# Where the Mamba scan's operands come from: DMA spreads delta over the states, three PSUM tiles for the inputs, and GpSimd weights the inputs of 4 of 16 pairs

## The chip, the cores and the metric

The kernel runs on one core of a Trainium2 chip. The metric is the device time of one execution in microseconds (us); lower is better. A core has five engines that run their own instruction streams in order and wait for each other through semaphores: TensorE (PE, matrix multiply; PEld in the profile is its weight load), VectorE (DVE), ScalarE (ACT), GpSimd (POOL) and SyncE (SP, which here only issues DMAs). SBUF is the working memory of 128 partitions; PSUM is where PE writes, and in this kernel POOL works on SBUF only.

## The reference, cut to what matters

Four layers work on four images of 56 x 56 pixels with 128 channels: windowed attention, a Mamba block (the change is here), additive attention with a mixture of experts, and softmax attention with a second mixture. All is fp32. The Mamba layer takes each image row as a sequence of 56 steps:

```
u = silu(conv(h @ in_w)) ; dt, Bm, Cm = split(u @ xw)
delta = softplus(dt @ dtw + dtb)        # one number per step and channel, 256 channels
A = -exp(A_log)                         # 256 channels x 16 states
h_t = exp(delta_t * A) * h_(t-1) + delta_t * u_t * B_t       # 256 x 16 states
y_t = sum over states of h_t * C_t
out = (y + u * D) * silu(res) @ out_w   # and twice: NL = 2 such layers
```

## The kernel before, in words

**Tiling of the Mamba stage (function layer1).** A chunk is 448 steps: 8 image rows of one image (CH = 448, 7 chunks an image). One *block* is one chunk in one of the two Mamba layers, so there are 4 x 7 x 2 = 56 blocks. A block has 256 channels x 16 states = 4096 recurrences, which are 32 tiles of 128 partitions (8 channels x 16 states) by 448 steps. They are worked two at a time: a *pair* is 128 x 896, and a block has PAIRS = 16 pairs, the stage 896.

**One pair before.** The order is written by hand, in a loop over p (lines 864 to 875), and each engine takes its instructions in that order:

- `select` (L739): PE makes `a` = delta times rate, spread over states (`decays`, L723, against the table `A_pick`), and `u` = delta*u spread over states (`spread_inputs`, L732, against the 0/1 table `pick`). `a` is one PSUM tile of two banks, `u` two such tiles. `decays` is for pair p+1 where `spread_inputs` is for pair p; the two use different groups of 32 rows of PE.
- ACT makes E = exp(a) from PSUM to SBUF (L748).
- `inputs` (L753): DVE multiplies u by B in place, in PSUM.
- `scan` (L760): DVE runs the recurrence over E (SBUF) and u (PSUM) into `hs` (SBUF, 7 buffers); then POOL multiplies hs by C in place (L765).
- `sums` (L771): PE adds up the states of two pairs into `y`, issued at every odd p for the pairs p-5 and p-4.

**Around a block.** `mamba_pre` (L877) prepares the next block at fixed pair numbers of the running one: conv (L889), silu (L901), the projection (L907), delta, B and C (L918 to L932), du = delta*u on POOL (L936, after pair 8), and two POOL memsets that put 1e30 at the first step of each row, so that exp gives 0 and the recurrence restarts (L939). `gate` (L787, POOL), `project` (L796, L804) and `pass_on` finish the previous block. m and y in PSUM have one bank each; with a (2 banks) and u (4) all eight banks are in use.

**Queues.** All DMAs are issued by SP, in an order that a scheduler sets; the other engines' order is as written. In the Mamba stage SP has nothing to do. Ahead of it, in layer 0, SP loads everything: the tables, the weights (`layer1_weights`, L605 to 639), and then images 1 to 3 (`load_image`, L127). Image 1 is normalised early in layer 0 (L184).

## Time and profile before

| what | value |
| --- | --- |
| three timed runs | 7893.22, 7884.90, 7877.51 us; median 7884.9 |
| span of the profiled execution | 7883.1 us, 1.8 us under that median |
| busy over the span: PE, DVE, ACT, POOL | 6718.3, 6070.7, 4990.0, 2552.6 us |
| first and last scan start (L760) | 650.8 and 3529.3 us |
| one pair in between | (3529.3 - 650.8) / 895 = 3.216 us |
| one block of 16 pairs | 51.46 us |
| DMA traffic | 102.35 MB, mean 13 GB/s |

The page gives busy time by engine, then 40 slices of the span with busy shares in tenths, the chain of work that ended last, and groups of instructions with their count, busy time, the mean duration of one in ns, and the idle time of the engine just before them with what released it. The view by windows gives each engine's busy time in a stretch, the granted PE clock, the DMA engines' mean busy share and their GB/s. The timeline gives start, duration, engine, line, operation and operands; x4 means four merged instructions, and brackets show idle time ahead and who ended it.

### The profile page before, as it was taken

The page shows a single profiled execution, that of the slowest core. Times are in us where ns is not written, and L with a number is a line of the kernel's source. Part 1 is how long each engine was busy: PE and PEld are TensorE (multiplying, and loading weights), DVE is VectorE, ACT ScalarE, POOL GpSimd, SP SyncE. Part 2 cuts the span into 40 slices and gives each one's busy share as a digit, 9 for nine tenths or more (in the row PEclk, how much of TensorE's full clock was granted, in tenths as well). Part 3 has the DMA queues.
Part 4 walks back from the last instruction along what each step waited for, and adds up shares of the span by engine and source line. Part 5 has one row for each costly group of instructions (what it writes and reads, how often), then busy time and mean ns, then how long its engine had stood idle before and what let it go on. Part 6 is the DMA issues. An engine that isn't in the chain of part 4 may idle for free.

```text
span 7883.1 us, 105890 instructions
## 1 busy us (share of the span) xinstructions
PE 6718.3 (85%) x41081; PEld 2672.6 (34%) x41081; DVE 6070.7 (77%) x10241; ACT 4990.0 (63%) x4903; POOL 2552.6 (32%) x1911
## 2 busy tenths in 40 slices
PE   7888989998999899987777777777777889999999
PEld 3452333333333333322222222222222344444544
DVE  5787999999999999997877887877787755344434
ACT  4455555555555655548998899899889953333332
POOL 4455777777777777760000000000001000000000
PEclk8998999999999999999999999899999989999999
DMA  3000000000000000000000000000003101210000
GB/s 63 6 2 1 1 1 1 1 1 1 1 1 1 1 1 1 1 3 2 1 1 1 5 1 1 1 5 1 1 32 114 47 6 47 91 57 5 5 5 6
DMA packets 86479, 102.35 MB, mean 13 GB/s; under 512 B 21368, under 2 KB 51414, under 8 KB 85463
## 3 DMA queue, kind: packets, MB, share of 16 engines
q1 hardware_dynamic: 85975, 95.58, 4.2%
q8 instruction: 322, 5.28, 0.3%
q14 instruction: 182, 1.49, 0.1%
HBM read 85.28 MB, written 10.29 MB: 12 GB/s over the span
## 4 chain that ended last, share of the span: by engine, by line
PE 35%; DVE 33%; ACT 20%; issue 7%; POOL 1%; DVEq 0%; DMA 0%; ACTq 0%; SPq 0%; POOLq 0%
DVE hs L760 17%; ACT th L1149 13%; PE q L1707 7%; PE o L1718 7%; DVE u L753 6%; PE s L1160 6%; DVE th L1140 4%; PE o L1187 2%; PE pe L1872 2%; ACT E L748 2%; PE a L723 2%; PE m L889 2%; DVE e L488 1%; ACT L748 1%; PE y L771 1%
## 5 line engine op out<-in xcount | busy, mean ns | idle before, releaser
L1149 ACT ACTIVATE th<-th 128x3136 f32<-128x3136 f32 (+12 forms) x1120 | 2293.6, 2093 | 194.6 <-DVE th L1140 138.4
L1140 DVE TENSOR_SCALAR th<-fT,g 128x784 f32<-128x784 f32 (+6 forms) x3920 | 1918.4, 556 | 482.2 <-PE s L1160 449.9
L765 POOL TENSOR_TENSOR hs<-hs,bc 128x896 f32<-128x896 f32 x896 | 1867.3, 2084 | 793.5 <-DVE hs L760 761.3
L1160 PE MATMUL s<-th,place 128*32 128x392 f32 (+7 forms) x14336 | 1489.2, 492 | 667.8 <-ACT th L1149 664.8
L760 DVE TENSOR_TENSOR_SCAN hs<-E,u 128x896 f32<-128x896 f32 x896 | 1810.1, 2020 | 117.9 <-ACT E L748 1.9
L748 ACT ACTIVATE E<-a 128x896 f32<-128x896 f32 x896 | 821.5, 917 | 806.3 <-PE u L732 333.7
L723 PE MATMUL a<-delta,A_pick 32*128 32x448 f32 x3584 | 983.2, 601 | 148.0 <-ACT E L748 140.4
L753 DVE TENSOR_TENSOR u<-u,bc 128x896 f32<-128x896 f32 x896 | 964.2, 1076 | 63.9 <-PE u L732 63.5
L732 PE MATMUL u<-du,pick 32*128 32x448 f32 x3584 | 975.2, 601 | 35.8 <-DVE hs L760 35.7
L1160 PEld LDWEIGHTS s<-th,place 128*32 128x32 f32 (+1 forms) x14336 | 425.7, 111 | 1612.1 <-ACT th L1149 1082.4
L1712 ACT ACTIVATE e<-q,shift 128x448 f32<-128x448 f32 (+1 forms) x700 | 441.4, 633 | 748.6 <-PE q L1707 748.2
L1178 POOL TENSOR_TENSOR e<-e,later 112x112 f32<-112x112 f32 x112 | 80.2, 716 | 2311.9 <-ACT e L1171 1670.1
L1718 PE MATMUL o<-e,xk 128*128 128x448 f32 (+1 forms) x1400 | 653.1, 548 | 25.7 <-ACT oT L1693 25.7
L1877 DVE SCALAR_TENSOR_TENSOR X<-pe,r_gate,X 112x128 f32<-112x128 f32 x896 | 314.0, 351 | 455.3 <-PE pe L1872 419.7
L1707 PE MATMUL q<-xT 128*128 128x448 f32 (+1 forms) x1400 | 654.7, 550 | 2.3 <-ACT e L1712 2.2
L723 PEld LDWEIGHTS a<-delta,A_pick 32*128 32x128 f32 x3584 | 295.7, 188 | 697.4 <-ACT E L748 466.5
L771 PE MATMUL y<-hs,sum 128*32 128x448 f32 x3584 | 443.9, 566 | 4.4 <-POOL hs L765 4.4
L1187 PE MATMUL o<-e,xa 112*128 112x392 f32 (+5 forms) x1024 | 424.3, 537 | 1.1 <-POOL e L1178 1.1
L1718 PEld LDWEIGHTS o<-e,xk 128*128 128x128 f32 (+1 forms) x1400 | 262.2, 191 | 310.5 <-issue 275.5
L732 PEld LDWEIGHTS u<-du,pick 32*128 32x128 f32 x3584 | 295.5, 188 | 200.0 <-DVE hs L760 183.9
L1707 PEld LDWEIGHTS q<-xT 128*128 128x128 f32 (+1 forms) x1400 | 249.0, 189 | 238.1 <-issue 213.0
L1806 POOL MEMSET lc_xa<- 112x4 f32 x28 | 3.1, 110 | 889.5 <-DVE lc_xa L1800 519.5
(254 smaller groups left out, 7186.2 us busy)
## 6 DMA issues: line engine op xcount, KB each, us to landing
wide<-in_L_ffn_weight SPq DMA_DIRECT2D x64, 1024.0 KB
X<-in_x SPq DMA_DIRECT2D x8, 784.0 KB
out<-X SPq DMA_DIRECT2D x28, 224.0 KB
M<-wide SPq DMA_DIRECT2D x4, 784.0 KB
wide<-M SPq DMA_DIRECT2D x4, 784.0 KB
e_edge<-dtab SPq DMA_DIRECT2D x42, 49.0 KB
cw<-in_L_conv_conv_w SPq DMA_DIRECT2D x4, 256.0 KB
c_h<-in_L_ffn_weight SPq DMA_DIRECT2D x16, 64.0 KB
```

The source lines that it names most:

```text
L723: nc.tensor.matmul(halves(to)[:, k], w["A"][own, order[j][2], f, q, :], pre[j]["delta"][own, f], start=True, stop=True,)
L732: nc.tensor.matmul(halves(to)[:, k], w["pick"][own, q, :], pre[j]["du"][own, f], start=True, stop=True,)
L748: nc.scalar.activation(E[p + 1], t, AF.Exp)
L753: nc.vector.tensor_mul(v, v, pre[p // PAIRS]["bc"][:, 0:1].to_broadcast([P, 2, CH]))
L760: nc.vector.tensor_tensor_scan(flat, E.pop(p), V.pop(p), 0.0, op0=ALU.mult, op1=ALU.add)
L765: nc.gpsimd.tensor_mul(HS[p], HS[p], bc[:, 1:2].to_broadcast([P, 2, CH]))
L1140: nc.vector.tensor_scalar(th[i][:, blk, lo:hi], fT[j][:, lo:hi], im[order[j][0]]["g"][:, at : at + 1], None, op0=ALU.add,)
L1149: nc.scalar.activation(own, own, AF.Tanh)
L1160: nc.tensor.matmul(ps[j, J][QW * blk : QW * blk + rows, h, lo:hi], place[:, off : off + rows], z[:, blk, h * HALF + lo : h * HALF + hi], s ...
L1187: nc.tensor.matmul(po[j][:, h, lo:hi], im[b]["xa"][:, J, :], e[:, h * HALF + lo : h * HALF + hi], start=(J == 0), stop=(J == t + ((h + 1) ...
L1707: nc.tensor.matmul(ps[:n, :CH], xT[b][:, k : k + n], xT[b][:, c * CH : (c + 1) * CH], start=True, stop=True,)
L1718: nc.tensor.matmul(po[b, c], xk[b][:n, t, :], es.pop((b, c, t))[:n], start=(t == 0), stop=(t == N - 1))
```

## The change

It does four things. The state index becomes the outer part of the partition number (`% DG`, `// DG` instead of `// DS`, `% DS` in the tables), so that the 8 channels of a tile are 8 rows, repeated 16 times. `mamba_pre` writes delta and du of each block to DRAM (8 DMAs), and `fetch` reads for each pair 8 rows x 3584 bytes into 128 partitions (one DMA of 448 KB, each row read 16 times): delta for 12 pairs, du for 4. For the 12 pairs ACT applies the rate as a per-partition scale, exp(rate * delta), in two halves in place in SBUF, and PE makes only u. For the pairs 0, 3, 7 and 12 of a block PE makes only a, ACT exponentiates it in place in PSUM, and POOL multiplies the fetched du by B in SBUF; the scan then reads E from PSUM and the input from SBUF. PSUM's six banks are three tiles of one kind. `rate` is a new table, loaded in layer 0 by 32 DMAs of 8 x 32 single numbers, ahead of images 1 to 3.

```diff
+POOL_PAIRS = (0, 3, 7, 12)
+DG = P // DS
+ROW_END = 8
...
-        pick[:, q, :] = (p % HD // 8 == q)[:, None] & (p[None, :] // DS == p[:, None] % 8)
-        back[p, q, 8 * q + p // DS] = 1.0
+        pick[:, q, :] = (p % HD // DG == q)[:, None] & (p[None, :] % DG == p[:, None] % DG)
+        back[p, q, DG * q + p % DG] = 1.0
...
+        w["rate"] = self.t(wp, [P, NL, DI // DG], "rate")
+        by_state = a["L1_conv_A_log"].rearrange("l (g d) n -> n l d g", d=DG)
+            for n in range(DS):
+                own = slice(n * DG, (n + 1) * DG)
+                for l in range(NL):
+                    nc.sync.dma_start(out=w["rate"][own, l], in_=by_state[n, l])
...
+        def rate():
+            nc.scalar.activation(w["rate"], w["rate"], AF.Exp)
+            nc.vector.tensor_scalar(w["rate"], w["rate"], -1.0, None, op0=ALU.mult)
...
-            ps_a = ctx.enter_context(tc.tile_pool(name="l1_a", bufs=1, space=PSUM))
-            ps_u = ctx.enter_context(tc.tile_pool(name="l1_u", bufs=2, space=PSUM))
+            dr = ctx.enter_context(tc.tile_pool(name="l1_dram", bufs=2, space=DRAM))
+            ps_u = ctx.enter_context(tc.tile_pool(name="l1_u", bufs=3, space=PSUM))
...
+            on_pool = lambda p: p % PAIRS in POOL_PAIRS
+            inside = lambda p: 0 <= p < n_pairs
+            def fetch(p):
+                j, f, q, r0 = place(p)
+                if on_pool(p):
+                    to, of = V, pre[j]["du_dram"]
+                    to[p] = self.t(sm, [P, 2 * CH + ROW_END], "V")[:, : 2 * CH]
+                else:
+                    to, of = D, pre[j]["delta_dram"]
+                    to[p] = self.t(sm, [P, 2 * CH + ROW_END], "E", bufs=5)[:, : 2 * CH]
+                rows = of[f, r0 // 2, q * DG : (q + 1) * DG].rearrange("d k t -> d (k t)")
+                nc.sync.dma_start(
+                    out=to[p],
+                    in_=rows.unsqueeze(0).to_broadcast([DS, DG, 2 * CH]),
+                )
             def select(p):
-                if 0 <= p + 1 < n_pairs:
-                    t = two_banks(ps_a, "a")
-                    decays(p + 1, t)
-                if 0 <= p < n_pairs:
-                    V[p] = two_banks(ps_u, "u")
-                    spread_inputs(p, V[p])
-                if 0 <= p + 1 < n_pairs:
-                    E[p + 1] = self.t(sm, [P, 2 * CH], "E", bufs=3)
-                    nc.scalar.activation(E[p + 1], t, AF.Exp)
-            def inputs(p):
-                if 0 <= p < n_pairs:
+                j, f, q, r0 = place(p)
+                u = two_banks(ps_u, "u")
+                if on_pool(p):
+                    decays(p, u)
+                    nc.scalar.activation(u, u, AF.Exp)
+                    E[p] = u
+                    return
+                spread_inputs(p, u)
+                V[p] = u
+                E[p] = D.pop(p)
+                for k in range(2):
+                    e = halves(E[p])[:, k]
+                    g = (f * QG + r0 + k) * QG + q
+                    rate = w["rate"][:, order[j][2], g : g + 1]
+                    nc.scalar.activation(e, e, AF.Exp, scale=rate)
+            def inputs(p, eng):
+                if on_pool(p) == (eng is nc.gpsimd):
                     v = halves(V[p])
-                    nc.vector.tensor_mul(
+                    eng.tensor_mul(
                         v, v, pre[p // PAIRS]["bc"][:, 0:1].to_broadcast([P, 2, CH])
                     )
...
-                if p >= -2:
-                    select(p + 1)
-                if 0 <= p < n_pairs:
+                if inside(p + 4):
+                    fetch(p + 4)
+                if inside(p + 2):
+                    select(p + 2)
+                    inputs(p + 2, nc.gpsimd)
+                if inside(p + 1):
+                    inputs(p + 1, nc.vector)
+                if inside(p):
                     scan(p)
...
-                inputs(p + 1)
...
+            for of in ("delta", "du"):
+                to = r[of + "_dram"] = dr.tile([NHALF, 2, HD, 2, CH], F32, tag=of, name=of + "_dram")
+                for i in range(4):
+                    nc.sync.dma_start(
+                        out=to[:, i // 2, :, i % 2].rearrange("f c t -> c f t"),
+                        in_=r[of][i * HD : (i + 1) * HD],
+                    )
```

More of the change, by code (lines that the diff above doesn't have):

```diff
@@ L95, in host_constants @@
         "k_out": back_out,
-        "k_state": (p[None, :] % DS == np.arange(DS)[:, None]).astype(np.float32),
+        "k_state": (p[None, :] // DG == np.arange(DS)[:, None]).astype(np.float32),
         "k_pick": pick.reshape(P, QG * P),
@@ L624, in layer1_weights @@
         )
+        w["rate"] = self.t(wp, [P, NL, DI // DG], "rate")
+        by_state = a["L1_conv_A_log"].rearrange("l (g d) n -> n l d g", d=DG)
+        with nc.allow_non_contiguous_dma(reason="a small table, by state and channel"):
+            for n in range(DS):
+                own = slice(n * DG, (n + 1) * DG)
+                for l in range(NL):
+                    nc.sync.dma_start(out=w["rate"][own, l], in_=by_state[n, l])
         xw = self.load(
@@ L649, in rates @@
             nc.vector.scalar_tensor_tensor(
-                w["A"][:, l, f, q, :].rearrange("p (j n) -> p j n", n=DS),
-                w["pick"][:, q, :].rearrange("p (j n) -> p j n", n=DS), -1.0,
-                A[:, l, f, :].unsqueeze(1).to_broadcast([P, P // DS, DS]),
+                w["A"][:, l, f, q, :].rearrange("p (n j) -> p n j", n=DS),
+                w["pick"][:, q, :].rearrange("p (n j) -> p n j", n=DS), -1.0,
+                A[:, l, f, :].unsqueeze(2).to_broadcast([P, DS, DG]),
                 op0=ALU.mult, op1=ALU.mult,
@@ L664, in layer1_weights @@
         bind = lambda f, *args: lambda: f(*args)
-        steps = [lambda: nc.scalar.activation(A, A, AF.Exp)]
+        def rate():
+            nc.scalar.activation(w["rate"], w["rate"], AF.Exp)
+            nc.vector.tensor_scalar(w["rate"], w["rate"], -1.0, None, op0=ALU.mult)
+        steps = [lambda: nc.scalar.activation(A, A, AF.Exp), rate]
         steps += [
@@ L703, in layer1 @@
             h = {}
-            pre, yg, E, V, HS, py = {}, {}, {}, {}, {}, {}
+            pre, yg, E, D, V, HS, py = {}, {}, {}, {}, {}, {}, {}
             def hand_over(b, g):
@@ L848, in layer1 @@
                 add(last, at + 12, skip, j, 1)
-                head, tail = self.mamba_pre(pre, j, block, h, w, sm, m)
+                head, tail = self.mamba_pre(pre, j, block, h, w, sm, m, dr)
                 for steps, to in ((head, first), (tail, last)):
@@ L874, in layer1, with mamba_pre @@
                     step()
-                inputs(p + 1)
-    def mamba_pre(self, pre, j, block, h, w, sm, m):
+    def mamba_pre(self, pre, j, block, h, w, sm, m, dr):
         nc = self.nc
```

## The prediction

> **What bounds the kernel now.** I read the page first (busy shares, slices), then the windows of the Mamba stage, then its groups of instructions and its timeline.

> ```profile
> DVE  5787999999999999997877887877787755344434
> ```
> ```profile
> 1500.00:2000.00 500.00, 455.77 (x2324) 157.98 (x2316) 476.53 (x333) 277.69 (x341) 363.86 (x211) 0.96 0.00 1
> 2000.00:2500.00 500.00, 463.84 (x2344) 162.84 (x2344) 477.27 (x321) 286.02 (x347) 370.06 (x211) 0.96 0.00 1
> ```
> Columns of the windows: length, then busy us of PE, PEld, DVE, ACT, POOL, granted PE clock, DMA share, GB/s. DVE is busy 95% through the stage; POOL is idle a quarter of it, ACT 43%, the DMA engines all of it. PE shows 92%, but see below: much of that is order, not need.

> ```profile
> 2002.92 1.07 DVE L753 TENSOR_TENSOR u<-u,bc 128x896 f32<-128x896 f32 x1
> 2004.13 2.02 DVE L760 TENSOR_TENSOR_SCAN hs<-E,u 128x896 f32<-128x896 f32 x1
> 2006.07 1.07 DVE L753 TENSOR_TENSOR u<-u,bc 128x896 f32<-128x896 f32 x1
> ```
> Read start to start. The multiply holds DVE for 1.21 us (the scan waits for its result); the scan for 1.94, because the next multiply, which doesn't need it, starts 0.09 before its end. So a pair costs 3.15, a block 16 x 3.145 = 50.3, plus 0.95 of other DVE work (the remaining groups of 1000 to 3300 us: 42.6 us over 44.7 blocks) = 51.3. Measured: 51.46. DVE alone sets the stage's 56 x 51.46 = 2882 us.

> **The change, part by part, for one block.**

> *DVE.* Four multiplies leave. The other twelve now stand before the scan of the pair ahead, which doesn't need them; by the 0.09 overlap above they hold DVE 1.07 - 0.09 = 0.98, not 1.21. Sum: 16 x 1.94 + 12 x 0.98 + 0.95 = 43.8. If the 0.23 of wait stays, 46.5. I take 43.8: the scan-to-multiply step shows independent neighbours.

> *POOL.*
> ```profile
> 2006.29 2.08 POOL L765 TENSOR_TENSOR hs<-hs,bc 128x896 f32<-128x896 f32 x1 [1.05 <-DVE hs L760]
> 2008.33 1.13 POOL L787 TENSOR_TENSOR yg<-yg,sres 128x448 f32<-128x448 f32 x1
> 2009.44 2.08 POOL L765 TENSOR_TENSOR hs<-hs,bc 128x896 f32<-128x896 f32 x1
> ```
> The bracket on the first line is the slack: over 1 us in most pairs. Back to back, hs costs 2.04, yg 1.11, du with its memsets 2.24 (2024.04 to 2026.28). Now: 16 x 2.04 + 2 x 1.11 + 2.24 + 0.06 = 37.2. Added: 4 x 2.04 = 8.2 for the same shape. Sum 45.4: **POOL is the new longest engine**, 1.6 above DVE. The multiplies are worth 4 x 0.98 = 3.9 on DVE and cost 8.2 on POOL; they pay because POOL had 14 us idle.
> [...]

> *PE.* A pair's u alone takes 0.95 (four instructions at 2032.62, the next work at 2033.57); a and u together took 0.96 where they ran on different rows at once (2025.04 to 2026.00). So dropping one of the two saves PE little. Floor: 16 x 0.95 + 8 x 0.89 (sums) + 6.8 (conv) + 1.8 (xw) + 3.8 (dbl) + 1.9 (res) + 1.9 (D) + 3.4 (projection) = 42.0. `select(p+2)` waits for the third PSUM tile, released by scan p-1; DVE wants u after scan p. Laying the PE work out by pair number, PE is late for pair 4 by about 1.0 (convs at pairs 0 and 1 fill it, and pair 3 has no multiply to cover) and within 0.4 at pairs 2, 8, 9 and 13.

> *ACT.* 12 x (2 x 0.63 - 0.92) = +4.1 (0.63 is the row of a half with a per-partition operand, L897), on 29.4: 33.5 of 46. It works two pairs ahead, so the table loads stay covered, tightly at pair 9 after softplus.

> *DMA and SP.* Per block 16 fetches of 459 KB and 0.92 MB written: 8.3 MB in 46 us = 180 GB/s. Rows, none of this very kind:
> ```profile
> 228.00:229.00 1.00, 1.00 (x14) 0.59 (x12) 0.64 (x1) 0.78 (x2) 0.61 (x1) 1.00 0.55 139
> 229.00:230.00 1.00, 1.00 (x18) 0.40 (x18) 1.00 (x2) 0.80 (x1) 1.00 (x1) 1.00 0.45 123
> ```
> This is one load of 256 KB that reads one 2 KB row into all 128 partitions (`cw`, issued at 227.25): 1.0 us of all engines together, 262 GB/s while they run, all landed 2.75 us after issue. The 512-byte rows of the images reach 217 to 225. So the engines have room (share about 0.69 at 262). SP issues 24 DMAs x 0.35 = 8.4 of 46. The fetches are issued several pairs ahead (five E buffers), so their landing (2.75, plus 0.8 for the larger size = 3.5) is hidden, except at the block's start: du on POOL (after pair 8), 8 writes (2.8), landing 1.9 (the last `dtab` store at 25.02, the load that waits for it at 26.88), fetch 3.5, one fetch queued ahead 1.8: 10.0. POOL meanwhile has hs 9 to 13, one input multiply and yg: 13.5. Cover 3.5; if it is lost, each us over it stalls POOL once per block, 56 us in all.

> *Sum of the stage.* POOL 45.4 and DVE 43.8 with PE's 1.0 on it = 44.8 are nearly level and coupled: an input multiply stands in POOL's queue two pairs before its scan, so POOL can lag by only two to three pairs. I add 1.3 to the longer for that and for the waits, a choice of mine (today DVE loses 0.2 of 51.3 with POOL slack; two nearly level engines must lose more, and PE's lateness alone is 1.0): **46.7**. Saved 56 x (51.46 - 46.7) = 267. Bounds: 45.4 (339 saved) and 49.5 (110 saved, rival 1).

> *Layer 0.*
> ```profile
> 65.65 0.98 PE L184 MATMUL m<-ident,X 112*128 112x112 f32 x4 [13.89 <-DMA X<-in_x]
> ```
> Every engine already stands for 14 us because image 1 comes late. The 32 `rate` loads are ahead of it in SP's queue; the small loads after it (L977, L978) follow each other in 0.46: +15, with DMA work of 8192 four-byte packets beside it. Bounds: 32 x 0.31 = 10, and by the page's mean packet (4.2% of 16 x 7883 us over 85975 packets = 62 ns) 32 us on 16 engines, 63 if only half take part. I take 16, unhidden. The pipeline's first fill has cover: du ends at 626.8, the first scan is at 650.8, and writes, fetch and multiply need 12.

> *Total.* 7883.1 - 267 + 16 = 7632 of span; with the 1.8 us around it **7634**.

> **Rivals.**

> 1. *PE or ACT, or the chain at the block's start, takes the place of DVE* (a smaller gain). For: PE's floor of 42.0 has waits on ACT in it, ACT runs 5 us in one go around its table loads, cover at the start is 3.5. With 48 to 49.5 a block: 110 to 194 saved, 16 to 20 lost: 7705 to 7800. Against: three PSUM tiles, two pairs of lead.

> 2. *The fetches don't come fast enough* (slower). Place: the 16 DMA engines; a block is 128 packets of 3584 bytes for each and 32 half as long, 144 in all. It costs nothing until 144 packets take longer than 46.7 (324 ns each) and makes the kernel slower from 51.2 (355 ns, 161 GB/s). At 380 ns a block is 54.7: +181 + 16 = 8080. For: no row has 8 rows read 16 times each from freshly written DRAM, for 2.6 ms on end. Against: `cw` read one row 128 times at 125 ns for 2 KB (1.0 x 16 / 128), 219 ns for 3584 bytes by proportion; even the 512-byte rows reach 217 GB/s.
> [...]

> 3. *DVE and POOL hold each other up.*
> ```profile
> L225 DVE TENSOR_TENSOR gn_q<-gn_q,gn_ve 128x1 f32<-128x1 f32 x3 | 5.9, 1955 | 0.1
> ...
> L753 DVE TENSOR_TENSOR u<-u,bc 128x896 f32<-128x896 f32 x714 | 768.4, 1076 | 15.7 <-PE u L732 15.4
> ```
> A one-element multiply of two SBUF operands took 1.96 us beside a busy POOL, 0.16 in layer 0 with POOL idle. If the four scans with their input in SBUF were held like that, 4 x 2 = 8 a block: 54.7, 8080 again. Against: they still have one operand in PSUM, as L753 has, and that is not held. The few such small operations cost at most 20 us in all.

> **How the numbers follow.** Forecast 68%: 7560 to 7700, likeliest 7634. Rival 1 17%: 7705 to 7800. Rival 2 8%, rival 3 4%: near 8080. Left 3%: below 7560, or no change. The range 7560 to 7800 leaves out rivals 2 and 3 and that rest. Faster by over 0.2% (16 us, about what a measurement can tell from no change) 86%, within 2%, slower 12%.

> **What would show it.** Right: POOL busy about 97% in the stage, DVE about 93%, DVE's waits before scans ended by POOL's V at pairs 0, 3, 7 and 12; scans still 2.02 and POOL's multiplies still 2.08; DMA share 0.5 to 0.7 at 180 GB/s; the idle time before L184 near 30. Wrong: DVE's idle time ended by a DMA (rival 2) or by u of PE or E of ACT (rival 1), scans longer than 2.02 (rival 3), POOL's idle time before its input multiply ended by a DMA (the block's start).

## The result and the profile after

The changed kernel is **slower**: 7961.18 us median of 4 runs (7955.61 to 7963.58) against 7889.06 (7877.51 to 7897.53) of the kernel before; ratio 1.0092, 95% interval 1.0077 to 1.0106. The profiled execution has a span of 7960.8 us, 77.7 more than before. First and last scan stand at 659.7 and 3601.4: the Mamba stage took 2941.7 us, 63.2 more, and a block (2941.7 / 895 x 16) 52.6 us instead of 51.46. Another 8.9 us are lost ahead of the first scan, 5.6 behind the last.

Of the page after, the busy tenths of PE and DVE and the granted PE clock in 40 slices (the Mamba stage is slices 4 to 18):

```profile
PE   6888888888888888887777777777777889999999
...
DVE  5886888888888887887877887887787755444434
...
PEclk8997888788878887878999999999999989999999
```

DVE has fallen from 9 tenths to 8 in the stage, PE from 8 or 9 to 8, and the granted clock, 0.96 in the stage before, is at 7 or 8 tenths. The windows say it in figures (length; busy us of PE, PEld, DVE, ACT, POOL; granted PE clock, DMA share, GB/s):

```profile
1500.00:2000.00 500.00, 438.08 (x1660) 143.31 (x1660) 411.90 (x274) 299.45 (x447) 431.52 (x242) 0.82 0.61 156
2000.00:2500.00 500.00, 431.54 (x1660) 143.04 (x1657) 420.28 (x286) 304.56 (x455) 430.97 (x244) 0.83 0.61 157
```

No engine is full: PE 431 to 438 of 500, DVE 412 to 420, POOL 431. The fetches run at 156 to 157 GB/s. DVE's rows from 1000 to 3000 us show what it waits for (busy us, mean ns of one, then idle us just before them and who ended it):

```profile
L799 DVE TENSOR_TENSOR_SCAN hs<-E,u 128x896 f32<-128x896 f32 x455 | 899.6, 2004 | 0.7 <-ACT E L787 0.7
L792 DVE TENSOR_TENSOR u<-u,bc 128x896 f32<-128x896 f32 x453 | 491.8, 1086 | 284.3 <-PE u L748 282.8
L799 DVE TENSOR_TENSOR_SCAN hs<-u,V 128x896 f32<-128x896 f32 x151 | 303.9, 2012 | 0.0
```

VectorE stands 284.3 of 2000 us ahead of its multiply, nearly all of it for u, from PE. It does not wait for E of ACT (0.7), nor for V of POOL (0.0), and a scan with its input in SBUF takes 2.012 us like one with its input in PSUM (2.004).

PE's own groups in the same stretch:

```profile
L748 PE MATMUL u<-du,pick 32*128 32x448 f32 x1812 | 564.5, 683 | 37.9 <-DVE hs L799 31.9 <-DVE gn_mean L214 6.0
...
L961 PE MATMUL m<-dbl,dbl_w 32*128 32x448 f32 x298 | 200.9, 762 | 31.2 <-ACT bc L972 29.2 <-ACT delta L967 1.9
...
L950 PE MATMUL m<-us,xw 128*128 128x448 f32 x152 | 96.9, 777 | 113.3 <-ACT us L944 113.3
...
L843 PE MATMUL m<-ow,yg 128*112 128x128 f32 x312 | 67.4, 403 | 30.6 <-ACT bc L972 30.6
```

The same two places in the kernel before:

```profile
L732 PE MATMUL u<-du,pick 32*128 32x448 f32 x2476 | 672.5, 599 | 21.5 <-DVE hs L760 21.3
...
L907 PE MATMUL m<-us,xw 128*128 128x448 f32 x156 | 69.1, 565 | 22.1 <-ACT us L901 22.0
```

Two things are new. The matmuls have become longer (u 683 ns, xw 777, where the kernel before has 599 and 565), and PE stands 113.3 us (before: 22.1) for `us` of ScalarE ahead of the xw matmuls. How the two hang together is seen in the timeline (start, duration, engine, line):

```profile
1987.57 3.35 PE L950 MATMUL m<-us,xw 128*128 128x448 f32 x4 [3.09 <-ACT us L944]
...
2002.08 1.07 DVE L792 TENSOR_TENSOR u<-u,bc 128x896 f32<-128x896 f32 x1
...
2002.87 0.64 PE L961 MATMUL m<-dbl,dbl_w 32*128 32x448 f32 x1 [1.14 <-ACT bc L972]
...
2003.06 2.01 DVE L799 TENSOR_TENSOR_SCAN hs<-E,u 128x896 f32<-128x896 f32 x1
...
2004.99 1.07 DVE L792 TENSOR_TENSOR u<-u,bc 128x896 f32<-128x896 f32 x1
...
2005.83 3.35 PE L835 MATMUL m<-yg,ow 128*128 128x448 f32 x4 [1.50 <-ACT bc L972]
...
2009.11 1.62 PE L748 MATMUL u<-du,pick 32*128 32x448 f32 x4
...
2010.79 1.10 DVE L792 TENSOR_TENSOR u<-u,bc 128x896 f32<-128x896 f32 x1 [2.81 <-PE u L748]
```

The longest pause comes once a block, ahead of xw: 3.09 us before 1987.57, and 113.3 us in 38 pauses over the stretch. Shorter ones follow. PE was done with its queue at 2001.73 and stood 1.14 us until ScalarE, with a table load and a softplus (2000.15 to 2002.40) ahead of it, had copied `bc` and freed the one m bank. At 2003.54 its clock falls to half (below); after a second pause (2004.33 to 2005.83) the four projection matmuls take 3.35 us, the next pair's u 1.62 instead of 1.02, and DVE, which had kept its pace until then (2002.08 to 2003.06 to 2004.99: 0.98 and 1.93, where 0.98 and 1.94 were predicted), stands 2.81 us for that u.

The clock itself, in 1-us windows of the same stretch, those in which it changes:

```profile
1986.00:1987.00 1.00, 0.00 (x0) 0.00 (x0) 1.00 (x2) 1.00 (x2) 0.20 (x1) 0.74 0.03 11
...
1996.00:1997.00 1.00, 1.00 (x11) 0.20 (x8) 1.00 (x1) 0.66 (x2) 1.00 (x1) 0.64 0.00 0
...
2003.00:2004.00 1.00, 1.00 (x6) 0.28 (x6) 1.00 (x2) 1.00 (x1) 1.00 (x1) 0.77 0.00 0
...
2010.00:2011.00 1.00, 1.00 (x8) 0.16 (x8) 0.21 (x1) 0.00 (x0) 1.00 (x1) 0.82 0.71 170
...
2020.00:2021.00 1.00, 0.14 (x2) 0.14 (x2) 0.96 (x3) 0.98 (x2) 0.05 (x1) 0.80 1.08 255
...
2030.00:2031.00 1.00, 1.00 (x2) 0.00 (x0) 0.96 (x2) 0.15 (x1) 1.00 (x2) 0.58 0.08 32
```

The trace's clock records hold no other value than 1.00 and 0.50, so the clock column is a mixture of these two: 0.77 at 2003 means that the clock fell at 2003.54, 0.82 at 2010 that it rose at 2010.36. Read like this it is half from 1986.48 to 1996.72, from 2003.54 to 2010.36 and from 2020.60 to 2030.84: 10.24, 6.82 and 10.24 us. In the kernel before, the same reading of 2000 to 2056 gives a single stretch of 3.40 us.

### The profile page after: what moved, and what is told of

Its sections match the earlier page's. It is cut to its first block, busy times and chain, and to the rows that moved or that the text cites. A ratio compares the mean times of both kernels' runs of the same rounds, so it can differ in the third digit from the quotient of the medians.

```text
span 7960.8 us, 102547 instructions
## 1 busy us (share of the span) xinstructions
PE 6650.7 (84%) x37497; PEld 2608.3 (33%) x37497; DVE 5789.7 (73%) x10018; ACT 5145.1 (65%) x5576; POOL 2997.3 (38%) x2135
## 4 chain that ended last, share of the span: by engine, by line
PE 34%; ACT 16%; DVE 9%; issue 6%; POOL 0%; DMA 0%; SPq 0%; ACTq 0%; DVEq 0%; POOLq 0%
ACT th L1199 13%; PE q L1757 7%; PE o L1768 7%; PE s L1210 6%; DVE th L1190 5%; PE o L1237 3%; PE pe L1922 2%; PE u L748 2%; PE m L932 1%; DVE hs L799 1%; PE y L810 1%; PE m L961 1%; ACT e L1221 1%; DVE X L1927 1%; ACT E L787 1%
## 5 line engine op out<-in xcount | busy, mean ns | idle before, releaser
L799 DVE TENSOR_TENSOR_SCAN hs<-E,u 128x896 f32<-128x896 f32 x672 | 1328.6, 2004 | 0.7 <-ACT E L787 0.7
L792 DVE TENSOR_TENSOR u<-u,bc 128x896 f32<-128x896 f32 x672 | 729.8, 1086 | 477.8 <-PE u L748 474.8
L748 PE MATMUL u<-du,pick 32*128 32x448 f32 x2688 | 853.1, 694 | 55.6 <-DVE hs L799 49.6
L787 ACT ACTIVATE E<-E,rate 128x448 f32<-128x448 f32 x1344 | 810.8, 660 | 3.2 <-DMA E<-delta_dram 1.8
L810 PE MATMUL y<-hs,sum 128*32 128x448 f32 x3584 | 505.6, 638 | 4.5 <-POOL hs L804 4.5
L792 POOL TENSOR_TENSOR V<-V,bc 128x896 f32<-128x896 f32 x224 | 467.1, 2085 | 8.4 <-DMA V<-du_dram 8.4
L799 DVE TENSOR_TENSOR_SCAN hs<-u,V 128x896 f32<-128x896 f32 x224 | 450.8, 2012 | 0.0
L748 PEld LDWEIGHTS u<-du,pick 32*128 32x128 f32 x2688 | 269.7, 217 | 448.0 <-issue 218.5
L777 ACT ACTIVATE u<-u 128x896 f32<-128x896 f32 x224 | 202.5, 904 | 301.3 <-PE u L739 301.1
L961 PE MATMUL m<-dbl,dbl_w 32*128 32x448 f32 x448 | 311.5, 784 | 41.6 <-ACT bc L972 37.5
```

Of the source, the lines that this page charges most:

```text
L748: nc.tensor.matmul(halves(to)[:, k], w["pick"][own, q, :], pre[j]["du"][own, f], start=True, stop=True,)
L787: nc.scalar.activation(e, e, AF.Exp, scale=rate)
L792: eng.tensor_mul(v, v, pre[p // PAIRS]["bc"][:, 0:1].to_broadcast([P, 2, CH]))
L799: nc.vector.tensor_tensor_scan(flat, E.pop(p), V.pop(p), 0.0, op0=ALU.mult, op1=ALU.add)
L810: nc.tensor.matmul(py[j, f][r * HD : (r + 1) * HD, :], w["sum"][:, q, :], HS[p + r // 2][:, r % 2], start=False, stop=(q == QG - 1),)
```

## The experiments

Four theories stood against each other. **CLOCK**: pauses of PE of 1 to 2 us bring its granted clock down to half, the slow PE is late with u, and DVE waits. **ORDER**: PE's stream waits behind ScalarE's exponentials and table loads, whatever the clock. **TRAFFIC**: the new DMA traffic slows the other engines. **COUPLING**: DVE and POOL hold each other up through the four multiplies on POOL.

The table gathers the runs; each ratio is to runs of the kernel before on the same chip, in turn with them. "Stage block" is from the first and the last scan's start. The next columns are per block, from the window 1000 to 3000 us (scans / 16 blocks in it): PE busy less fillers, the fillers' own time, PE idle, DVE idle; then the granted clock. PE busy, fillers and idle add up to the block by construction, so they split a time; by themselves they don't prove a cause.

| kernel | time (us), ratio to before with interval | stage block | PE own | fillers | PE idle | DVE idle | clock |
| --- | --- | --- | --- | --- | --- | --- | --- |
| before | 7889.06 | 51.5 | 47.1 | | 4.6 | 2.5 | 0.96 |
| after | 7961.18, 1.0092 [1.0077, 1.0106] | 52.6 | 45.5 | | 7.3 | 8.6 | 0.83 |
| e1 exponentials last | 7753.27, 0.9831 [0.9816, 0.9845] | 48.8 | 41.7 | | 7.3 | 4.9 | 0.91 |
| e2 fillers in the pauses | 7693.75, 0.9757 [0.9742, 0.9771] | 47.6 | 39.2 | 5.6 | 3.1 | 3.8 | 0.96 |
| e3 before + traffic | 7901.70, 1.0019 [1.0010, 1.0028] | 51.9 | 46.2 | | 5.9 | 2.9 | 0.95 |
| e4 no pair on POOL | 7916.21, 1.0034 [1.0019, 1.0049] | 51.6 | 45.1 | | 6.7 | 3.8 | 0.88 |
| e5 fillers where PE is busy | 7942.22, 1.0069 [1.0054, 1.0084] | 52.1 | 41.9 | 5.3 | 5.5 | 8.5 | 0.92 |
| e6 e1 and e2 | 7699.27, 0.9764 [0.9748, 0.9780] | 47.5 | 39.1 | 5.6 | 3.1 | 3.8 | 0.96 |
| e7 e6, rate loads late | 7676.26, 0.9735 [0.9721, 0.9750] | 47.8 | 39.1 | 5.6 | 3.2 | 4.0 | 0.96 |
| e8 only the fillers at pair 3 | 7755.05, 0.9837 [0.9822, 0.9851] | 49.0 | 40.9 | 2.5 | 5.5 | 4.9 | 0.92 |
| e9 e2, rate loads late | 7686.45, 0.9747 [0.9731, 0.9764] | 47.7 | 39.3 | 5.5 | 3.1 | 3.9 | 0.96 |
| e10 before + fillers | 7956.55, 1.0091 [1.0076, 1.0106] | 52.4 | 43.8 | 6.0 | 2.8 | 3.4 | 0.99 |
| e11 e9, no pair on POOL | 7866.72, 0.9975 [0.9965, 0.9984] | 51.0 | 41.5 | 6.0 | 3.6 | 3.3 | 0.92 |
| e12 e9, three pairs on POOL | 7668.33, **0.9726** [0.9712, 0.9741] | 47.4 | 39.1 | 5.7 | 2.7 | 2.5 | 0.98 |
| e13 no function tables changed | 7673.81, 0.9729 [0.9709, 0.9749] | 47.4 | 43.2 | | 4.4 | 3.5 | 0.89 |
| e14 fillers, a quarter of the columns | 7820.95, 0.9924 [0.9909, 0.9939] | 49.9 | 42.1 | 2.7 | 5.6 | 6.2 | 0.89 |

**e1, exponentials at the end of the iteration.** `select(p+2)` keeps PE's part; ScalarE's exponentials of that pair are issued behind the block's own steps, so that the copies for which PE waits go first.

```diff
                 for step in last.get(p, []):
                     step()
+                if inside(p + 2):
+                    exps(p + 2)      # the activations that stood in select(p + 2)
```

> The changed kernel with one thing moved: ScalarE's exps of pair p+2 stand at the end of an iteration, behind the copies that free PE's one bank m, instead of ahead of them. Theory ORDER (PE stands still because its in-order stream waits for ScalarE, which does exps and table loads first; in the changed kernel PE waits 5.0 us a block for ACT): those waits fall by 2 us a block or more, block 52.6 to 50.5 or less, time 7840 or less. Theory CLOCK (what costs is the granted clock of 0.83, which drops when PE stands still): idle time falls a little and the clock rises a little, 7850 to 7930. Theory TRAFFIC (157 GB/s of DMA in the stage slow PE or its clock): nothing changes, 7945 to 7975, clock 0.83.

Measured 7753.27, 208 less than the changed kernel. That is ORDER's number (7840 or less) without its sign, since PE's waits did not fall; CLOCK's forecast, a small gain to 7850 to 7930, was missed. The window 1000 to 3000, first of the kernel after, then of this one:

```profile
1000.00:3000.00 2000.00, 1724.56 (x6678) 575.35 (x6676) 1672.94 (x1136) 1207.52 (x1803) 1724.38 (x968) 0.83 0.61 157
```

```profile
1000.00:3000.00 2000.00, 1701.26 (x7188) 576.57 (x7186) 1799.59 (x1219) 1308.51 (x1952) 1856.42 (x1045) 0.91 0.68 169
```

PE's idle time per block is the same, 7.3 us, while its own work went from 45.5 to 41.7 and the clock from 0.83 to 0.91. Nothing was taken off PE and nothing added, so the 3.8 us are PE running faster; 56 blocks of 3.8 are 213 us, the whole gain. What changed is how the pauses are cut up (the one ahead of xw falls from 113.3 us in 38 to 76.8 in 41, those ahead of dbl rise from 31.2 us to 93.0), not their sum.

**e2, fillers.** Six matmuls with zero weights per block, which add nothing to y, three at pair 3 and one each at pairs 6, 7 and 8, where PE stands.

```diff
+            def fill(p):
+                for _ in range({3: 3, 6: 1, 7: 1, 8: 1}.get(p % PAIRS, 0)):
+                    for y in py.values():
+                        nc.tensor.matmul(
+                            y, w["zero"], w["pick"].rearrange("p q c -> p (q c)")[:, :CH],
+                            start=False, stop=False,
+                        )
...
+                fill(p)
                 if p % 2 and 0 <= p - 5 < n_pairs:
                     sums(p - 5)
```

> The changed kernel with six extra matmuls of zero weights a block (0.95 us each when the clock is full) added into y, put where PE waits for ScalarE: three in pair 3 and one each in pairs 6, 7 and 8. The sum is unchanged. CLOCK: PE no longer falls idle for over a microsecond there, the granted clock of the stage rises from 0.83 to 0.93 or more, DVE's idle time before its multiply falls by half, block 49 to 51, time 7780 to 7870. ORDER: the clock rises, but PE still comes late, block 52 to 54, time 7930 to 8040. TRAFFIC: the clock stays near 0.83 and the time rises by up to 5.7 us a block.

Measured 7693.75, 267 less than the changed kernel, more than expected. PE's groups of this kernel:

```profile
L750 PE MATMUL u<-du,pick 32*128 32x448 f32 x2001 | 547.3, 594 | 38.2 <-DVE hs L801 32.2 <-DVE gn_mean L214 6.0
...
L820 PE MATMUL y<-pick,zero_w 128*128 128x448 f32 x498 | 231.8, 574 | 0.0
...
L961 PE MATMUL m<-us,xw 128*128 128x448 f32 x164 | 72.6, 565 | 18.9 <-ACT us L955 18.4
```

u is at 594 ns again and xw at 565; the wait for `us` fell from 113.3 to 18.9 us although ScalarE's work is the same, because PE now works through it. The fillers of pair 3 stand ahead of xw, where the changed kernel has its pause of 3 us; this kernel's timeline there:

```profile
2003.17 2.52 PE L820 MATMUL y<-pick,zero_w 128*128 128x448 f32 x6
...
2006.94 1.77 PE L961 MATMUL m<-us,xw 128*128 128x448 f32 x4 [0.36 <-ACT us L955]
2008.64 1.02 PE L750 MATMUL u<-du,pick 32*128 32x448 f32 x4
```

The fillers (2003.17) run through the pause; the following u (2008.64) takes 1.02 us. More work on the engine that is late made the kernel 3.4% faster. This run alone doesn't tell the clock from a mere shift of PE's stream; e1 above and e5 below do more.

**e3, the traffic alone.** The kernel before, plus the writes of delta and du and one fetch of 448 KB for every pair, whose contents aren't used.

```diff
+                if 0 <= p + 4 < n_pairs:
+                    fetch(p + 4)          # into E[p + 4], overwritten by its exponentials
```

> The kernel before, with the change's DMA traffic and nothing else of it: delta and du written to DRAM for each block, and for each pair a fetch of 448 KB into the E tile (5 buffers), which ScalarE then overwrites with exp(a) as before. TRAFFIC: the clock of the stage falls from 0.96 towards 0.83 and the block from 51.5 to 52.5 or more, time 7945 or more. CLOCK and ORDER: the clock stays at 0.96 and the time within 0.2% of the kernel before, 7875 to 7905.

Measured 7901.70, ratio 1.0019: 159 GB/s beside the kernel before cost 15 us. TRAFFIC falls as the main cause. It is not without effect: PE's pauses grow from 4.6 to 5.9 us a block, which costs little where DVE is the bound. What that adds in the changed kernel isn't separated here; e12 below runs at a clock of 0.98 with 174 GB/s.

**e4, no pair on POOL.** `POOL_PAIRS = ()`.

> The changed kernel with no pair on GpSimd: all 16 pairs take the fetched delta, ScalarE's two half exps, and VectorE's multiply. It separates the split between DVE and POOL from the rest. ORDER and CLOCK: ScalarE does 4 x 0.33 us more a block and PE the same work, so PE is as late as before or later, block 52 to 54, time 7930 to 8040, although DVE's own sum is 47.7. If instead the coupling of DVE and POOL costs (rival COUPLING): below 51.5 a block, time 7900 or less.

VectorE's sum is here 16 x (1.94 + 0.98) + 0.95 = 47.7. Measured 7916.21, between the two expectations: 45 us better than the changed kernel, still slower than before, with the clock at 0.88. Giving up POOL's part wins 45 of the 327 us between the forecast of 7634 and the measured 7961, so it isn't the main cause.

**e5, the same fillers where PE is busy anyway.** `{0: 2, 1: 2, 2: 2}` instead of `{3: 3, 6: 1, 7: 1, 8: 1}`.

> The changed kernel with the same number of zero-weight matmuls as in the run with fillers (six per block into y), but issued at pairs 0, 1 and 2, where PE has work queued, not at pairs 3, 6, 7 and 8, where it stands still. CLOCK (PE's pauses take its granted clock down, and slow PE makes VectorE wait for u): the pauses stay or only shift, so the stage's mean clock rises little, to at most 0.88, and the time lies between that of the changed kernel and 150 us above it: 7930 to 8110. The rival, that six more matmuls per block help wherever they stand (by delaying y, or by spacing the streams): 7690 to 7740, as with fillers in the pauses.

Measured 7942.22, 19 less than the changed kernel: fillers as such help little, their place does. But CLOCK's own number was missed: the clock rose to 0.92, not to at most 0.88. The fillers delay PE's stream, ScalarE is ready more often when PE comes, and the pause for `us` goes from 113.3 to 17.0 us. PE's own work fell by 3.6 us a block and its pauses by 1.8, and the fillers ate 5.3: nearly a draw. So the clock alone doesn't decide; a high clock has to be had without work ahead of a u that is due.

**e6, both edits.**

> The changed kernel with both edits that helped: exponentials at the end of the iteration (7753 alone) and fillers in PE's pauses (7694 alone). CLOCK with ORDER as a second cause: the fillers hold the clock at 0.96 or more and the moved exponentials take ScalarE's waits off PE; VectorE's idle time before the mul falls below 60 us in 2000, the block goes to 46.0 to 47.2, and the time to 7600 to 7670. The rival, that both edits cure one and the same thing (the pauses): no better than fillers alone, 7680 to 7720.

Measured 7699.27, the rival's number: both cure one thing. DVE's rows show what the moved exponentials add:

```profile
L806 DVE TENSOR_TENSOR_SCAN hs<-E,u 128x896 f32<-128x896 f32 x502 | 992.8, 2004 | 60.9 <-ACT E L794 60.9
L799 DVE TENSOR_TENSOR u<-u,bc 128x896 f32<-128x896 f32 x502 | 541.4, 1078 | 81.5 <-PE u L750 81.5
```

The wait for u falls from 137.2 us (e2) to 81.5, and 60.9 of waits for E take its place: exponentials that are issued last come late for the scan.

**e7 and e9, the rate loads behind the images.**

```diff
-                    nc.sync.dma_start(out=w["rate"][own, l], in_=by_state[n, l])
...
+            self.rate_loads()        # the same 32 loads, after those of the images
             self.layer2_loads()
```

> As the run with both edits, with the 32 small rate loads issued behind the images' loads, and layer 0's rate step as the last of its loading steps. If these loads in front of the images are what delays the first scan (659.7 in the changed kernel, 650.8 before), image 1 is waited for some 14 us again instead of 25, the first scan comes at 648 to 652, and the time is 8 to 12 us below that of the run with both. The rival, that the loads' own share of the queue's time is owed wherever they stand: within 4 us of it.

> The changed kernel with the fillers in PE's pauses and with the rate loads behind the images, without the moved exponentials. The fillers alone gave 7694, both edits with the late loads 7676. If the two gains (clock and image 1) simply add: 7672 to 7688. If the late loads need the moved exponentials: 7690 to 7700. Less than 7665 would say that moving the exponentials costs time once the clock is held.

Measured 7676.26 (23 below e6, more than expected) and 7686.45 (7 below e2, as expected). The first scan came at 649.7 and 648.7, where the changed kernel has 659.7: the loads cost some 10 us, and only because they stand in front. The rest of e7's 23 lies within the spread of single runs (7671 to 7687 against 7685 to 7704).

**e8 and e14, the dose.** e8 keeps the three fillers at pair 3; e14 keeps all places with a quarter of the columns (`y[:, : CH // 4]`).

> The changed kernel with half the fillers: only the three at pair 3, none at pairs 6, 7 and 8. CLOCK: the pause ahead of the dbl matmuls is filled, the later ones are not; the clock lies between 0.83 and 0.96, near 0.90, and the time between the two, 7760 to 7860. If one pause alone does the harm: within 20 us of 7694 (it is the one at pair 3) or of 7961 (it is a later one).

> The changed kernel with the same six fillers a block in the same places, but over a quarter of the columns (112 of 448), so about 1.4 us a block of PE work instead of 5.6. If the clock follows the share of the pauses that is filled, a quarter of the gain of 267: 7870 to 7920, clock 0.85 to 0.88. If it is enough that PE does anything in each pause: 7690 to 7760, clock 0.94 or more.

e8: 7755.05 at 0.92, just below what was expected: 45% of the fillers' PE time (2.5 of 5.6) for 77% of the gain (206 of 267); the pause at pair 3 is the dearest. By the timeline of e2 it is the pause ahead of xw, not the one ahead of dbl that the expectation names. e14: 7820.95, between both expectations. The short fillers took 332 ns each, not a quarter of 574, so they fill 2.7 of 5.6 us, 48%, and bring 140 of 267, 52%. With all places kept, the gain goes with the time that is filled; e8 shows that the place counts as well.

**e10, the fillers in the kernel before.**

> The kernel before with the very same fillers. CLOCK with PE as the bound of the changed kernel alone: before, the granted clock is 0.96 already and VectorE binds, so nothing is to be won, and the fillers add about 5.6 us of PE work to a block that has 4.7 of PE pauses: 7870 to 7960. The rival, that such fillers speed up any version of this kernel: 7750 or less.

Measured 7956.55, as expected: 71 us worse. The clock rises from 0.96 to 0.99 and brings nothing; the six matmuls cost. The cure belongs to the changed kernel. In the profiled executions the stage is 55 of the 72 us longer (first scan at 647.8, last at 3581.4), the start 3 shorter, and 20 lie behind the last scan; these runs don't say why.

**e11 and e12, POOL's share with the clock held.** e9 with `POOL_PAIRS = ()` and with `(0, 7, 12)`.

> As the run with fillers and late rate loads, with all 16 input multiplies on VectorE and none on POOL. VectorE's sum is then 16 x 2.92 + 0.95 = 47.7 a block, just the 47.6 that the kernel with fillers takes with four of them on POOL. If VectorE binds, with waits of 1 to 2 us on top: a block of 48.7 to 49.7 and 7735 to 7800. If PE is still what binds, the multiplies on POOL are worth nothing: 7670 to 7700.

> As the run with fillers and late rate loads, with three pairs on POOL (0, 7 and 12; pair 3 goes back to VectorE): VectorE's sum 44.8, POOL's 43.4 instead of 43.8 and 45.4, and pair 4's u gets the cover of pair 3's multiply. If the near tie of VectorE and POOL takes the rest of the time (47.6 against 45.4): 7630 to 7660. If PE's waits take it: within 12 us of the run with four pairs.

e11: 7866.72, 180 worse than e9, beyond both expectations and more than VectorE's sum says (a block of 51.0; VectorE is busy 47.7 of it, as the sum has it, and waits 3.3). PE waits for scans to free its PSUM tiles there (106 us in 2000 ahead of u), and the clock is at 0.92; how these divide is open. In the changed kernel as it stands, all 16 multiplies on VectorE are worth 45 us (e4); with the fillers in place they cost 180 (e11 against e9).
e12: 7668.33, between the two expectations: better than four pairs by 18, and the fastest of all runs, 2.7% below the kernel before. Its window and its multiply:

```profile
1000.00:3000.00 2000.00, 1885.01 (x7927) 642.63 (x7925) 1894.16 (x1299) 1357.39 (x2052) 1826.22 (x1034) 0.98 0.71 174
```

```profile
L800 DVE TENSOR_TENSOR u<-u,bc 128x896 f32<-128x896 f32 x547 | 591.0, 1080 | 84.7 <-PE u L756 84.7
```

The clock is at 0.98, and DVE waits for u 84.7 of 2000 us instead of 284.3.

**e13, no changes of function table.** In the changed kernel ScalarE makes 150 table loads of 1.28 us in 2000 us, at silu, at softplus and at the exp that follows them. This kernel applies other functions in their place, and none of the 150 is left in its trace.

```diff
-            nc.scalar.activation(r[to], r[of], AF.Silu)
+            nc.scalar.activation(r[to], r[of], AF.Identity)
-            nc.scalar.activation(r["delta"], r["delta"], AF.Softplus)
+            nc.scalar.activation(r["delta"], r["delta"], AF.Exp)
```

> The changed kernel without ScalarE's changes of function table in the Mamba stage: it applies the identity where the reference has silu, and exp where it has softplus, so its output is another function. Nothing is added to PE. If the table loads (150 of 1.28 us in 2000 us, 5.1 a block) make PE's pauses, the pauses fall below 4 us a block, the clock rises to 0.92 or more without any filler, and the time is 7660 to 7780. If the trips from PE to ScalarE and back through the one m bank make them, whatever the tables: clock below 0.88 and 7850 to 7950.

Measured 7673.81: without a single filler, all of the gain. Its window and PE groups:

```profile
1000.00:3000.00 2000.00, 1815.11 (x7420) 599.10 (x7418) 1853.42 (x1257) 1119.92 (x1841) 1911.99 (x1077) 0.89 0.71 174
```

```profile
L748 PE MATMUL u<-du,pick 32*128 32x448 f32 x2020 | 534.1, 644 | 55.3 <-DVE hs L799 48.6 <-DVE gn_mean L214 6.0
...
L961 PE MATMUL m<-dbl,dbl_w 32*128 32x448 f32 x338 | 199.2, 673 | 0.0
...
L950 PE MATMUL m<-us,xw 128*128 128x448 f32 x172 | 76.1, 565 | 67.5 <-ACT us L944 67.5
```

The waits ahead of dbl are gone (31.2 to 0.0), those for `us` fell from 113.3 to 67.5. So ScalarE's chain, of which the table loads are 5.1 us a block, makes the pauses. The clock, though, rose only to 0.89 (0.92 or more was expected) and the pauses fell to 4.4, not below 4: part of this gain is shorter waiting (2.9 us a block), part a faster PE (2.4). PE's busy time alone doesn't give the clock: here PE is busy 1815 of 2000 us at 0.89, in the kernel before 1823 at 0.96 (last section). ORDER is therefore half of the matter here, and CLOCK what multiplies it.

## Why the prediction was wrong

- *DVE's sum, 43.8: right.* Its busy time is 1672.9 / 37.9 blocks = 44.2. The multiply stands 0.98 ahead of the scan and the scan 1.93 ahead of the next multiply, as worked out.
- *POOL's sum, 45.4: right* (1724.4 / 37.9 = 45.5), but it is not the longest engine that counts.
- *ACT, 33.5:* 1207.5 / 37.9 = 31.9, fewer than costed.
- *DMA:* right that it doesn't bind. 157 GB/s at a share of 0.61 is 257 while they run, close to the 262 read from `cw`; in e12 174 GB/s. There ScalarE waits 95.4 of 2000 us for a fetch, and none of it reaches VectorE (0.3 us for E). Rival 2 falls, with e3 as the test.
- *The block's start, cover 3.5:* right, POOL never waits there:

```profile
L792 POOL TENSOR_TENSOR V<-V,bc 128x896 f32<-128x896 f32 x152 | 316.9, 2085 | 0.0
```

- *Rival 3, scans held by POOL:* falls, 2.012 us.
- *Rate loads, +16 unhidden:* the right place, too much. Image 1 is waited for 25.40 instead of 13.89 us, +11.5, and the first scan is 8.9 later. With the loads behind the images (e12) the wait is 13.56 again.

```profile
77.46 0.98 PE L189 MATMUL m<-ident,X 112*128 112x112 f32 x4 [25.40 <-DMA X<-in_x]
```

```profile
65.90 0.98 PE L189 MATMUL m<-ident,X 112*128 112x112 f32 x4 [13.56 <-DMA X<-in_x]
```

- *PE's floor of 42.0: the step that failed.* As work at full clock it was even too high (39.1 to 39.3 where the clock is held). It failed in two terms. I used the durations of a kernel that runs at 0.96 for one that would run at 0.83: the own work came out at 45.5. And I counted almost none of PE's pauses, which are 7.3 us a block: 5.2 of them end with ScalarE, 2.0 with VectorE. 45.5 + 7.3 is the block of 52.8 in that stretch; DVE's wait for u, costed at 1.0 at pair 4, is 7.5.
- *"It works two pairs ahead, so the table loads stay covered"* is where the second term was lost. That holds for the exponentials: DVE waits 0.7 of 2000 us for E. It doesn't hold for the chain PE to ScalarE to PE (xw, dbl, `bc`), where the loads stand between two matmuls and nothing runs ahead. In the kernel before, PE had a second expansion per pair to do meanwhile; it was busy 47.1 of a block, with pauses of 4.6 and the clock at 0.96. The change took that work away and left the chain. That the missing work is what let the clock fall is argued from this and from the fillers' effect (e2: 0.83 to 0.96); no run put the old work back.
- *Rival 1* named the mechanism, PE or ACT in DVE's place, at 48 to 49.5 a block. It priced the wait and not the clock, so it ended below 51.46; measured 52.6. The rival that ended on the other side was looked for in DMA and POOL.
- With the fillers alone (e2) the block is 47.6 and the time 7694, inside the forecast's 7560 to 7700; with the rate loads moved and three pairs on POOL as well (e12) it is 47.4 and 7668, where 46.7 and 7634 were forecast. The sums of the other engines were good enough; PE's two terms are the miss.

What stays open: how much of the loss is clock and how much is waiting can't be given as one number. e1 is nearly all clock (3.8 of 3.8 us), e13 is 2.4 of 5.2, and each feeds the other.

## What to carry to other kernels

Taking matmuls off an engine that is not the bound can make it the bound (here the block went from 51.46 to 52.6): look up what those matmuls were filling. Before the floor of PE is used, list its round trips through another engine in the new order, and price what is left of PE at half the clock as well where they leave it standing for 1 to 3 us: here pauses of 3.09 and 1.14 us went with a fall of the clock, one of 1.73 us didn't. If a kernel then comes out slower than its sums, look at the granted clock by stage first; moving the other engine's work, shortening its chain, or a few zero-weight matmuls in the pauses test that, one run each; no one of them settles it alone.

## What the runs showed of the hardware

Two falls have a pause of PE beside them: one of 3.09 us ahead of the fall at 1986.48 and across it, and one of 1.14 us ahead of that at 2003.54. Yet the length of a pause doesn't decide alone: ahead of the xw matmuls at 2046.49 PE stood 1.73 us and the clock stayed at 1.00. Nor does PE's busy time. In the 3.41 us before 2003.54 PE was busy 2.27 and the clock fell; from 2044.50 to 2047.92, with the pause of 1.73 us inside, it was busy 1.69 of 3.42 and the clock stayed. Over 1000 to 3000 us the order isn't the same either: PE busy 1823 us at a clock of 0.96 before, 1815 at 0.89 in e13; 1869 at 0.96 in e2, 1859 at 0.92 in e11. The two short stretches also differ in their matmuls: u and dbl (32 x 128) and sums (128 x 32) in the first, the four xw (128 x 128) and the end of the sums in the second. Whether that decides isn't shown: no run varied the rows by themselves, and the ends of matmuls in a profile are modelled.

A half-clock stretch is dear out of proportion: the pause of 1.14 us at 2001.73 was followed by 6.82 us at half speed, with a second pause of 1.50 us inside. From 1000 to 3000 us, 0.83 is a third of the time at half clock (668.8 of 2000).
